# The odd slot of a cross-attention loop: the values' product moved ahead of the scores, its casts ahead of the odd tile's exponentials

## The chip, the cores and the metric

The kernel runs on one core of a Trainium2 chip. Five engines work side by side, each on its own queue of instructions in the order in which the program gives them: TensorE (PE in the profile, its weight loads PEld), VectorE (DVE), ScalarE (ACT), GpSimd (POOL) and SyncE (SP, which here only issues DMAs). An instruction that has to wait for another engine holds up everything behind it on its own queue. The metric is device microseconds of one execution.

## The reference

For each of 4 batches, 2048 rows of 512 numbers attend to a context of 77 rows with 16 heads of width 32; a mask drops context rows; the result is projected, added to the input and normalised.

```python
qs = (q @ wq)...; ks_ = (k @ wk)...; vs = (v @ wv)...        # k = v = context, heads of 32
scores = einsum('bhqd,bhkd->bhqk', qs, ks_) / sqrt(32)
scores = where(mask, -inf, scores)
attn = einsum('bhqk,bhkd->bhqd', softmax(scores), vs)
out = attn.reshape(...) @ wo + q
return (out - mean(out)) / sqrt(var(out) + 1e-5) * gamma + beta
```

Everything is float32.

## The kernel before

The 8192 rows are cut into 64 tiles of 128 rows; two tiles make a block (its number is n), and tile u = 2n is its even, u + 1 its odd tile. Products that need float32 accuracy are made of three float32r products: each operand is split into a high part (a cast on ScalarE) and a low part (the difference, on VectorE or GpSimd).

What happens to one tile, with the function and the engine:

- `q_visit` (L160, TensorE, 12 matmuls): one quarter of the queries of a group of four tiles; `q_evac` (L177, VectorE) copies it out. The rows come by `load_xT` (SP), are split by `cast_xT` (L149, ScalarE) and `split_xT` (L153, GpSimd).
- `scores` (L284, TensorE, 64 small matmuls): the 16 heads, in four PSUM banks j = 0 to 3 with four heads each. A head uses 32 rows and 64 columns of the array.
- `maxima` (L298, VectorE): mask and row maximum of one head, bank by bank (the list `HEADS` is ordered by j); writes the tile's buffer `pbuf`.
- `exps` (L312, ScalarE): the exponential of one head and its sum. `recip` (L323, VectorE): the reciprocals of the 16 sums. `normalise` (L328, GpSimd).
- `transp` (L352, VectorE) turns the tile within blocks of 32, `regroup` (L364, SP) moves a whole block with 12 DMAs into the tile `PT`.
- `av` (L382, TensorE, 32 matmuls on 96 rows and 32 columns of the array): the values' product of a block, in two banks `pa`. `av_hi` (L413, ScalarE, two casts) and `av_lo` (L417, VectorE, two differences) split it.
- `o_proj` (L446, TensorE, 12 matmuls): the projection of one tile; `residual` (L455), `moments` (L460, L465 on VectorE, L469 to L472 on GpSimd), `scale` (L478, ScalarE), `affine` (L482, L483, GpSimd), `store` (L486, SP).

The order of the work is written out by hand (the scheduler keeps it). A loop with `u = 0, 2, ..., 52` holds an even and an odd slot; tiles 54 to 63 follow a written list, `ORDER`, which the change doesn't touch. Stages are offset: while tile u is scored, block n - 2 goes through `av`, and tiles u - 6 and u - 5 through `o_proj`. So the order on TensorE is, for each pair: scores of u, `o_proj` of u - 6, a query visit; scores of u + 1, `av` of block n - 2, `o_proj` of u - 5, a query visit.

All PSUM tiles share eight banks. A bank is given out in the order in which banks came free in the program's text: a tile takes the bank whose last reader stands earliest, and TensorE waits for that reader. `AH`, `AL`, `PT` and the transposed tile `B` have two buffers each, `pbuf` has three.

The mask of the next batch is prepared in three pairs of the loop by `mask_bias` (L264, L265) and, one pair later, by `mask_nan` (L269 to L271), all on VectorE, at the end of the even slot.

Of the kernel before, what the change touches and what calls it, by code (L numbers as in the profile page):

```python
# [19 lines left out]
H = 16  # L20
# [47 lines left out]
def xattn_layernorm(  # L68
# [26 lines left out]
    def bank(name):  # L95
        return ps.tile([P, 512], F32, tag="mm", name=name)
# [37 lines left out]
    def keys_of(h):  # L134
        return slice(TAIL_K, NK2) if h % 2 == 0 else slice(0, NK)
# [6 lines left out]
    def load_xT(g, c):  # L142
        fx[g, c] = sb.tile([P, 2, GRP], F32, tag="xtf", name=f"xtf_{g}_{c}")
        nc.sync.dma_start(fx[g, c], xT[g, :, c : c + 2])
# [29 lines left out]
    def q_evac(g, m):  # L174
        pq = qp.pop((g, m))
        if g:
            nc.vector.tensor_copy(qd[g][:, m, :], pq)  # L177
        else:
            nc.vector.tensor_copy(qd[0][:, m : m + 2, BLK:], pq.rearrange("p (m r) -> p m r", m=2))
# [94 lines left out]
    def scores(t):  # L274
        qs = qd[t // 4]
        nmax[t] = sb.tile([P, H], F32, tag="nm", bufs=3, name=f"nm_{t}")
        sums[t] = sb.tile([P, H], F32, tag="sum", bufs=3, name=f"sum_{t}")
        sc = scs[t] = [bank(f"sc_{t}_{j}") for j in range(GH)]
        for g in range(NG):
            for half in range(0, P, P // 2):  # L280
                for j in range(GH):
                    q = slice(HD * j, HD * (j + 1))
                    r0 = (t % 4) * P + half
                    nc.tensor.matmul(  # L284
                        sc[j][half : half + P // 2, g * NK : (g + 1) * NK],
                        qs[q, g, r0 : r0 + P // 2],
                        kct[q, g, t // TPB, keys_of(j)],
                        start=True,
                        stop=True,
                    )  # L290

    def maxima(t, lo, hi):
        pb = pbuf[t % NPB]
        mb = bat[t // TPB][0]
        nm = nmax[t]
        for h in HEADS[lo:hi]:
            g, j = divmod(h, GH)
            nc.vector.tensor_tensor_reduce(  # L298
                pb[:, h // 2, (h % 2) * NK : (h % 2 + 1) * NK],
                scs[t][j][:, g * NK : (g + 1) * NK],  # L300
                mb[:, t % TPB, keys_of(h)],
                -1.0,
                3.0e38,
                ALU.add,
                ALU.min,
                accum_out=nm[:, h : h + 1],
            )

    def exps(t, lo, hi):
        pb = pbuf[t % NPB]  # L310
        for h in HEADS[lo:hi]:
            nc.scalar.activation(  # L312
                pb[:, h // 2, (h % 2) * NK : (h % 2 + 1) * NK],
                pb[:, h // 2, (h % 2) * NK : (h % 2 + 1) * NK],
                AF.Exp,
                bias=nmax[t][:, h : h + 1],
                scale=-1.0,
                accum_out=sums[t][:, h : h + 1],
            )

    def recip(t):
        ris[t] = sb.tile([P, H], F32, tag="ri", bufs=3, name=f"ri_{t}")
        nc.vector.reciprocal(ris[t], sums[t])  # L323
# [51 lines left out]
    def av(b):  # L375
        pt = pts[b].rearrange("p i a (q t r) -> p i a q t r", q=NP, t=2)
        for i in range(2):
            pas[b, i] = bank(f"pa_{b}_{i}")
        for g in range(NG):
            for j in range(GH):  # L380
                h = g * GH + j
                nc.tensor.matmul(  # L382
                    pas[b, g // 2][HD * j : HD * (j + 1), (g % 2) * BLK : (g % 2 + 1) * BLK],
                    vsb[:, 2 * b // TPB, HD * h : HD * (h + 1)],
                    pt[:NK2, :, h % 2, h // 2].rearrange("p i t r -> p t i r"),
                    start=True,
                    stop=True,
                )
# [16 lines left out]
    def at_part(b, k, i, by_tile):  # L405
        if by_tile:
            return at[b][k][:, :, i * P : (i + 1) * P], pas[b, i].rearrange("p (m r) -> p m r", m=NG)
        return at[b][k][:, 2 * i : 2 * i + 2], pas[b, i].rearrange("p (m r) -> p m r", m=2)

    def av_hi(b, i, by_tile=False):  # L410
        if b not in at:
            at[b] = [sb.tile([P, NG, BLK], F32R, tag=t, name=f"{t}_{b}") for t in ("AH", "AL")]
        nc.scalar.copy(*at_part(b, 0, i, by_tile))  # L413

    def av_lo(b, i, by_tile=False):
        hv, pv = at_part(b, 0, i, by_tile)
        nc.vector.tensor_tensor(at_part(b, 1, i, by_tile)[0], pv, hv.bitcast(F32), ALU.subtract)  # L417


    def load_x(t):  # L420
        if t < NT - 8:
            od[t] = sb.tile([P, D], F32, tag="o", bufs=8, name=f"o_{t}")
        elif t < NT - 4:
            if not ends:
                ends.append(sb.tile([P, NC_D, GRP], F32R, tag="xth", name="o_end").bitcast(F32))
            od[t] = ends[0][:, t % 4]
        else:
            if t % 2 == 0:
                ends.append(sb.tile([P, 2, GRP], F32, tag="xtf", name=f"o_end_{t}"))
            od[t] = ends[-1][:, t % 2]  # L430
        nc.sync.dma_start(od[t], x[t * P : (t + 1) * P, :])
# [148 lines left out]
    def pieces(u):  # L580
        return casts.get(u) or [((u + 8) // 4, u % 4)] * (u + 8 < 4 * NGRP)

    evac = [(0, 0)]
    for u in range(0, 2 * CUT, 2):
        n = u // 2
        m, k = divmod(u, TPB)

        for q in pieces(u + 2):
            if u >= 4:
                load_xT(*q)  # L590
        for t in (u - 4, u - 3):
            if t >= 0:
                load_x(t)
        scores(u)
        maxima(u, 0, H // 2)
        for q in evac:
            q_evac(*q)
        maxima(u, H // 2, H)
        for q in pieces(u):
            cast_xT(*q)  # L600
        exps(u, 0, 3 * H // 4)
        for v in list(vd):
            values_evac(v)
        for q in pieces(u):
            split_xT(*q)
        if u == 0:
            mask_bias(0, slice(1, TPB))
            split_wv()
        if u >= 6:
            o_proj(u - 6)  # L610
        for v in {2: (0,), 4: (2, 3)}.get(u, ()):
            values(v)
        for q in visits(u):
            q_visit(*q)
        if u >= 6:
            residual(u - 6)
            moments(u - 6)
        if u == 4:
            transp(2)
        if u:  # L620
            transp(u - 1)
            regroup(n - 1)
        if u >= 8:
            scale(u - 8)
            scale(u - 7)
        exps(u, 3 * H // 4, H)
        if u >= 8:
            affine(u - 8)
        for q in visits(u):
            q_evac(*q)  # L630
        if u == 0:
            load_wo()
            nc.gpsimd.memset(ident, 0.0)
            nc.gpsimd.affine_select(ident, ident, [[-1, P]], ALU.not_equal, 1.0, base=0, channel_multiplier=1)
        if u == 2:
            split_wo(0)
            split_wo(1)
        if k == TPB - 6 and m + 1 < NB:
            load_mask(m + 1)
        if k == TPB - 4 and m + 1 < NB:  # L640
            mask_bias(m + 1)
        if k == TPB - 2 and m + 1 < NB:
            mask_nan(m + 1)

        scores(u + 1)
        maxima(u + 1, 0, 3 * H // 4)
        recip(u)
        maxima(u + 1, 3 * H // 4, H)
        exps(u + 1, 0, H // 4)
        normalise(u)  # L650
        if u >= 8:
            affine(u - 7)
        for v in list(vd):
            values_evac(v)
        if u >= 4:
            av(n - 2)
            av_hi(n - 2, 0)
            av_hi(n - 2, 1)
        exps(u + 1, H // 4, H)
        if u >= 5:  # L660
            o_proj(u - 5)
        if u >= 4:
            av_lo(n - 2, 0)
        if u >= 5:
            residual(u - 5)
        if u >= 4:
            av_lo(n - 2, 1)
        if u != 2:
            transp(u)
        for v in {2: (1,)}.get(u, ()):  # L670
            values(v)
        evac = visits(u + 1)
        for q in evac:
            q_visit(*q)
        if u == 2:
            load_xT(*pieces(4)[0])
        if u >= 5:
            moments(u - 5)
        if u == 0:
            mask_nan(0)  # L680
        if u == 2:
            split_wo(2)
            split_wo(3)
        recip(u + 1)
        normalise(u + 1)
        if u >= 8:
            store(u - 8)
            store(u - 7)
# [87 lines left out]
```

## Time and profile before

| | us |
|---|---|
| median of 3 runs | 534.55 (533.18 to 534.91) |
| profiled execution, its time | 533.62 |
| profiled execution, its span | 531.8 |
| busy PE, DVE, ACT, POOL | 514.6, 485.3, 459.4, 401.1 |
| granted TensorE clock, mean | 0.996 |

A span runs from the first to the last instruction; the time has the launch around it. Instructions on one engine are pipelined, so one may start while the one before still shows as busy: for what a group costs in a full queue one takes the distance from its start to the start of the next group. "sc" is the tile of scores, "pq" queries, "po" projection, "pa" the values' product.

### The profile page before, as it was taken

The numbers are of one execution on the slowest core, as the hardware profiler recorded it, in microseconds if no ns is written. First come the engines' busy times: TensorE is split into PE (matmuls) and PEld (weight loads), VectorE is DVE, ScalarE is ACT, GpSimd is POOL, SyncE is SP. The second block draws the span as 40 slices with busy tenths as digits, with TensorE's granted clock in tenths as the row PEclk, the third lists the DMA queues.
The fourth block names the chain that finished last, engine by engine and source line by source line (L and its number), as shares of the span: only waits on it lengthen the run. The fifth ranks groups of instructions, "written<-read, shape, count | busy, mean of one in ns | idle before, by whom it ended". The sixth has DMA issues, their size and how long they took to land.

```text
span 531.8 us, 20432 instructions
## 1 busy us (share of the span) xinstructions
PE 514.6 (97%) x6858; PEld 393.0 (74%) x6858; DVE 485.3 (91%) x2592; ACT 459.4 (86%) x2215; POOL 401.1 (75%) x363
## 2 busy tenths in 40 slices
PE   8999999999999999999999999999999999998994
PEld 6977677777777777777777777777777777775672
DVE  5689889999999899889998998889999989999897
ACT  5687799998899999998899999998899999998500
POOL 0626537998799988887899888888799988665751
PEclk9999999999999999999999999999999999999998
DMA  8934757888778788887778788779777865859844
GB/s 303 403 119 110 216 148 183 234 210 221 212 185 219 216 226 211 217 208 206 200 201 226 206 222 220 190 188 254 188 201 215 229 187 160 220 141 272 230 135 158
DMA packets 58712, 110.24 MB, mean 207 GB/s; under 512 B 9392, under 2 KB 11056, under 8 KB 58608
## 3 DMA queue, kind: packets, MB, share of 16 engines
q1 hardware_dynamic: 55424, 102.64, 70.2%
q0 software_dynamic: 2304, 5.24, 3.5%
q10 hardware_dynamic: 880, 1.05, 0.8%
q8 instruction: 55, 0.90, 0.7%
q14 instruction: 49, 0.40, 0.2%
HBM read 41.79 MB, written 16.78 MB: 110 GB/s over the span
## 4 chain that ended last, share of the span: by engine, by line
PE 29%; ACT 28%; DVE 26%; DMA 9%; issue 3%; SPq 3%; POOL 1%; DVEq 0%; ACTq 0%
ACT pbuf L312 23%; PE po L446 10%; PE pq L160 9%; DVE pbuf L298 7%; DVE B L352 5%; DMA PT<-B 4%; PE pa L382 3%; PE sc L284 3%; DVE q L177 3%; DMA o<-x 3%; ACT AH L413 3%; SPq L364 2%; DVE st L460 2%; ACT o L478 2%; PE pk L186 1%
## 5 line engine op out<-in xcount | busy, mean ns | idle before, releaser
L312 ACT ACTIVATE pbuf<-pbuf,nm 128x77 f32<-128x77 f32 x1024 | 353.2, 356 | 30.0 <-DVE nm L298 24.8
L312 ACT ACTIVATION_READ_ACCUMULATOR pbuf<-pbuf,nm 128x1 f32 x1024 | 201.4, 197 | 0.0
L328 POOL TENSOR_TENSOR pbuf<-pbuf,ri 128x1232 f32<-128x1232 f32 x63 | 142.9, 2270 | 58.2 <-DVE ri L323 44.5
L298 DVE CUSTOM_DVE_ANT_0 pbuf<-sc,mb 128x77 f32<-128x77 f32 x1024 | 168.8, 230 | 3.1 <-PE sc L284 3.1
L446 PE MATMUL po<-woh,AH 128*128 128x512 f32 x256 | 108.6, 424 | 0.0
L446 PE MATMUL po<-wol,AH 128*128 128x512 f32 x256 | 100.2, 391 | 0.0
L446 PE MATMUL po<-woh,AL 128*128 128x512 f32 x256 | 100.1, 391 | 0.0
L160 PE MATMUL pq<-xth,wqh 128*128 128x512 f32 (+1 forms) x256 | 98.5, 385 | 0.1
L160 PE MATMUL pq<-xtl,wqh 128*128 128x512 f32 (+1 forms) x256 | 97.9, 382 | 0.0
L160 PE MATMUL pq<-xth,wql 128*128 128x512 f32 (+1 forms) x256 | 97.9, 382 | 0.0
L352 DVE STREAM_TRANSPOSE B<-pbuf 128x1280 f32<-128x1280 f32 x64 | 95.5, 1493 | 2.5 <-POOL pbuf L328 1.8
L298 DVE DVE_READ_ACCUMULATOR2_ANT nm<- 128x1 f32 x1024 | 84.3, 82 | 0.0
L284 PEld LDWEIGHTS sc<-kct,q 32*64 32x64 f32 x4096 | 51.9, 130 | 23.6 <-issue 16.5
L153 POOL TENSOR_TENSOR xtl<-xtf,xth 128x1024 fp32r<-128x1024 f32 x28 | 67.1, 2398 | 2.8 <-ACT xth L149 2.8
L382 PE MATMUL pa<-PT,vsb 96*32 96x256 f32 x992 | 60.2, 381 | 7.5 <-DMA o<-x 1.9
L483 POOL TENSOR_TENSOR o<-o,bet 128x512 f32<-128x512 f32 x48 | 63.2, 1316 | 3.8
L446 PEld LDWEIGHTS po<-woh,AH 128*128 128x128 f32 x256 | 48.0, 187 | 23.2 <-DVE nm L298 6.2
L284 PE MATMUL sc<-kct,q 32*64 32x77 f32 x4096 | 62.5, 238 | 0.4 <-DVE vsb L228 0.4
L482 POOL TENSOR_TENSOR o<-o,gam 128x512 f32<-128x512 f32 x48 | 61.8, 1287 | 0.6 <-ACT o L478 0.3
L446 PEld LDWEIGHTS po<-woh,AL 128*128 128x128 f32 x256 | 48.1, 188 | 10.9 <-DVE AL L417 0.3
L160 PEld LDWEIGHTS pq<-xth,wqh 128*128 128x128 f32 x256 | 48.1, 188 | 10.5 <-PE pq L160 0.5
L446 PEld LDWEIGHTS po<-wol,AH 128*128 128x128 f32 x256 | 48.2, 188 | 9.5 <-issue 1.4
(106 smaller groups left out, 670.9 us busy)
## 6 DMA issues: line engine op xcount, KB each, us to landing
PT<-B SPq DMA_DIRECT2D x346, 128.0 KB
xtf<-xT SPq DMA_DIRECT2D x28, 512.0 KB
o<-x SPq DMA_DIRECT2D x56, 256.0 KB
out<-o SPq DMA_DIRECT2D x56, 256.0 KB
PT<-B POOLq DMA_DIRECT2D x21, 128.0 KB, 5.1
o_end<-x SPq DMA_DIRECT2D x8, 256.0 KB
out<-o_end SPq DMA_DIRECT2D x8, 256.0 KB
xtf<-xT SPq DMA_DIRECT2D x4, 256.0 KB
```

Of the source, the lines that this page charges most:

```text
L153: nc.gpsimd.tensor_tensor(l, fx.pop((g, c)), h.bitcast(F32), ALU.subtract)
L160: nc.tensor.matmul(pq, w[:, c, m * P : (m + 1) * P], r[:, c, rs], start=(n == 0), stop=(n == 11))
L177: nc.vector.tensor_copy(qd[g][:, m, :], pq)
L284: nc.tensor.matmul(sc[j][half : half + P // 2, g * NK : (g + 1) * NK], qs[q, g, r0 : r0 + P // 2], kct[q, g, t // TPB, keys_of(j)], start= ...
L298: nc.vector.tensor_tensor_reduce(pb[:, h // 2, (h % 2) * NK : (h % 2 + 1) * NK], scs[t][j][:, g * NK : (g + 1) * NK], mb[:, t % TPB, keys_ ...
L312: nc.scalar.activation(pb[:, h // 2, (h % 2) * NK : (h % 2 + 1) * NK], pb[:, h // 2, (h % 2) * NK : (h % 2 + 1) * NK], AF.Exp, bias=nmax[t ...
L328: nc.gpsimd.tensor_tensor(pv, pv, rv.to_broadcast((P, NP, 2, NK)), ALU.mult)
L352: nc.vector.transpose(bt.rearrange("p c q r -> p q c r"), pbuf[t % NPB].rearrange("p q (c r) -> p q c r", c=5),)
L382: nc.tensor.matmul(pas[b, g // 2][HD * j : HD * (j + 1), (g % 2) * BLK : (g % 2 + 1) * BLK], vsb[:, 2 * b // TPB, HD * h : HD * (h + 1)], ...
L446: nc.tensor.matmul(pos[t], a[:, c, rs], w[:, c, :], start=(first and c == 0 and n == 0), stop=(c == NC_D - 1 and n == 2),)
L482: nc.gpsimd.tensor_tensor(o, o, gam, ALU.mult)
L483: nc.gpsimd.tensor_tensor(o, o, bet, ALU.add)
```

## The change

In the even slot the last four exponentials of tile u join the first twelve, ahead of the two `scale`s. In the odd slot `recip(u)` is the first thing on VectorE. On TensorE `av` goes ahead of the scores of tile u + 1 (it stood behind them), and `av_hi` on ScalarE stands ahead of all exponentials of tile u + 1 (four of them stood ahead of it). The two `av_lo` on VectorE stand behind the fourth and the eighth of the odd tile's maxima (they stood around `residual(u - 5)`). Nothing is added or removed, no DMA is moved, and the list for the last ten tiles is as it was.

```diff
         for q in pieces(u):
             cast_xT(*q)
-        exps(u, 0, 3 * H // 4)
+        exps(u, 0, H)
         for v in list(vd):
             values_evac(v)
...
             scale(u - 8)
             scale(u - 7)
-        exps(u, 3 * H // 4, H)
         if u >= 8:
             affine(u - 8)
...
+        recip(u)
+        if u >= 4:
+            av(n - 2)
+            av_hi(n - 2, 0)
+            av_hi(n - 2, 1)
         scores(u + 1)
-        maxima(u + 1, 0, 3 * H // 4)
-        recip(u)
-        maxima(u + 1, 3 * H // 4, H)
-        exps(u + 1, 0, H // 4)
+        maxima(u + 1, 0, H // 4)
+        if u >= 4:
+            av_lo(n - 2, 0)
+        maxima(u + 1, H // 4, H // 2)
+        if u >= 4:
+            av_lo(n - 2, 1)
+        maxima(u + 1, H // 2, H)
         normalise(u)
         if u >= 8:
             affine(u - 7)
         for v in list(vd):
             values_evac(v)
-        if u >= 4:
-            av(n - 2)
-            av_hi(n - 2, 0)
-            av_hi(n - 2, 1)
+        exps(u + 1, 0, H // 4)
         exps(u + 1, H // 4, H)
         if u >= 5:
             o_proj(u - 5)
-        if u >= 4:
-            av_lo(n - 2, 0)
         if u >= 5:
             residual(u - 5)
-        if u >= 4:
-            av_lo(n - 2, 1)
         if u != 2:
             transp(u)
```

## The prediction

> **What bounds the kernel now.** I read the page's busy line, then the busy times of the loop's settled part, then TensorE's instructions in order of time, and last the waits of that part.
>
> ```profile
> PE 514.6 (97%) x6858; PEld 393.0 (74%) x6858; DVE 485.3 (91%) x2592; ACT 459.4 (86%) x2215; POOL 401.1 (75%) x363
> ...
> 88.50:423.80 335.30, 330.76 (x4578) 254.68 (x4579) 312.74 (x1735) 318.20 (x1526) 293.36 (x244) 1.00 0.80 213
> ...
> 278.90 0.95 PE L284 MATMUL sc<-kct,q 32*64 32x77 f32 x64
> 279.78 0.51 PE L446 MATMUL po<-woh,AH 128*128 128x512 f32 x1
> ...
> 282.65 0.39 PE L160 MATMUL pq<-xth,wqh 128*128 128x512 f32 x1
> ...
> 285.14 0.39 PE L160 MATMUL pq<-xth,wql 128*128 128x512 f32 x1
> 285.46 0.95 PE L284 MATMUL sc<-kct,q 32*64 32x77 f32 x64
> 286.62 1.93 PE L382 MATMUL pa<-PT,vsb 96*32 96x256 f32 x32 [0.21 <-DMA o<-x]
> 288.49 0.50 PE L446 MATMUL po<-woh,AH 128*128 128x512 f32 x1
> ...
> 291.36 0.39 PE L160 MATMUL pq<-xth,wqh 128*128 128x512 f32 x1
> ...
> 294.17 0.95 PE L284 MATMUL sc<-kct,q 32*64 32x77 f32 x64
> ...
> L382 PE MATMUL pa<-PT,vsb 96*32 96x256 f32 x708 | 43.0, 381 | 4.7 <-DMA o<-x 1.9 <-DMA xtf<-xT 1.1 <-PE sc L284 0.9
> ```
>
> The second line (columns: window, length, busy PE, PEld, DVE, ACT, POOL, clock, DMA share, GB/s) begins at one `av` and ends at another, 22 pairs later: 335.3 / 22 = 15.24 us a pair. TensorE is busy for 330.76 of it, and the last row has all the rest: the only idle time of TensorE in 22 pairs is 4.7 us ahead of `av`, 0.2 each time, whatever landed meanwhile. ACT is busy 318.2 / 22 = 14.5 a pair, DVE 14.2, POOL 13.3, and the DMA engines 0.80 of the time. So TensorE sets the pace.
>
> **The steady pair.** From start to start the rows give: scores to projection 0.88, projection 2.87, query visit 2.81, scores to `av` 1.16, `av` 1.87, projection 2.87, query visit 2.81, together 15.27. `av` behind scores costs 0.28 more than a projection behind scores: the idle 0.21 and 0.07 of overlap. What it costs behind a query visit, and scores behind `av`, the list of the last tiles shows once:
>
> ```profile
> 438.62 0.39 PE L160 MATMUL pq<-xth,wql 128*128 128x512 f32 x1
> 438.93 1.93 PE L382 MATMUL pa<-PT,vsb 96*32 96x256 f32 x32
> 440.80 0.95 PE L284 MATMUL sc<-kct,q 32*64 32x77 f32 x64
> 441.68 0.50 PE L160 MATMUL pq<-xth,wqh 128*128 128x512 f32 x1
> ```
>
> From the last query matmul to `av` it is 0.31, where to scores it is 0.32 (285.14 to 285.46); `av` to scores takes 1.87, as `av` to projection does; no idle time is noted at either seam. The new pair is thus 0.88 + 2.87 + 2.81 + 1.87 + 0.88 + 2.87 + 2.81 = 14.99. Between both ends for the 0.28 (all of it gone; all of it moved to another seam) I take gone, by these rows. 23 `av` from 88.52 to 423.79 give 4.7 / 22 + 0.07 = 0.28 each: **-6.3 us**.
>
> A rule of the Trainium skill speaks against it: "TensorEngine Tiling (Array Packing)", section Tiling Modes, Key Properties, says that a change of tiling mode drains TensorE, and the new order has as many changes of mode (five a pair) as the old one. By that rule the sum would be 0 in place of -6.3; the rows at 438.93 and 440.80 show such changes with no idle time, so I keep it as a rival.
>
> **Do the other engines follow at 14.99?** I lay out a pair, with 0 at the start of the even scores; TensorE then starts `o_proj` at 0.9, the query visit at 3.7, `av` at 6.6, the odd scores at 8.4, `o_proj` at 9.3, the visit at 12.2. Prices:
>
> ```profile
> 428.72 0.69 DVE L455 TENSOR_TENSOR o<-po,o 128x512 f32<-128x512 f32 x1 [1.54 <-PE po L446]
> 429.33 0.68 DVE L417 TENSOR_TENSOR AL<-pa,AH 128x512 fp32r<-128x512 f32 x1
> 429.93 1.50 DVE L352 STREAM_TRANSPOSE B<-pbuf 128x1280 f32<-128x1280 f32 x1
> 431.35 0.65 DVE L460 BATCH_NORM_STATS2 st<-o 128x6 f32<-128x512 f32 x1
> 432.04 0.18 DVE L465 BATCH_NORM_AGGREGATE mv<-st 128x2 f32<-128x6 f32 x1
> 432.14 0.22 DVE L323 RECIPROCAL ri<-sum 128x16 f32<-128x16 f32 x1
> ...
> 432.61 0.36 ACT L312 ACTIVATE pbuf<-pbuf,nm 128x77 f32<-128x77 f32 x1 [0.61 <-DVE nm L298]
> ...
> L298 DVE CUSTOM_DVE_ANT_0 pbuf<-sc,mb 128x77 f32<-128x77 f32 x706 | 116.3, 230 | 0.0
> ...
> 407.54 1.41 ACT o L478 x2
> ...
> 411.69 0.95 ACT AH L413 x2
> 412.64 4.12 ACT pbuf L312 x24
> ...
> 420.78 2.40 POOL L153 TENSOR_TENSOR xtl<-xtf,xth 128x1024 fp32r<-128x1024 f32 x1
> 423.14 1.28 POOL L482 TENSOR_TENSOR o<-o,gam 128x512 f32<-128x512 f32 x1
> ...
> 428.20 1.29 POOL L482 TENSOR_TENSOR o<-o,gam 128x512 f32<-128x512 f32 x1
> ```
>
> A maximum is 116.3 / 706 = 0.16 (16 are 2.6), `residual`, `av_lo` or a query copy 0.6, `transp` 1.4, `moments` 0.8, `recip` 0.1; 16 exponentials are 4.12 x 16 / 12 = 5.5.
>
> VectorE, odd slot: maxima once the scores are through at 8.4 + 0.95 = 9.4; with the two `av_lo` 3.8, to 13.1; `residual` 13.7, `transp` 15.2, `moments` 16.0, `recip` 16.1, which is 1.1 in the next pair. Even slot: 2.6 + 0.6 + 0.6 + 0.8 + 1.4 + 0.6, so `recip(u)` comes up at 7.7. From there VectorE stands idle until 9.4, 1.7 us: the 1.54 that it waited for `residual` at 428.72, moved. `recip(u)`, now at the head, holds up the maxima behind it, but they wait for the scores anyhow.
>
> ScalarE: the first exponential comes 0.5 after `recip` (432.14 to 432.61), so `exps(u)` runs 1.4 to 6.9, so that `recip(u)` needn't wait; `scale` to 8.4, `av_hi` to 9.3 (its product was issued by 8.4), `exps(u + 1)` from 9.7 (the scores' 9.4 and one maximum) to 15.2, `cast_xT` 0.95 to 16.2 = 1.2. It fits, with 0.2 to spare.
>
> GpSimd: `affine(u - 8)` now waits for `scale` behind 16 exponentials instead of 12: 6.9 + 0.7 = 7.6, to 10.3 (2.65 by 423.14 and what follows it), `normalise(u)` to 12.5, ahead of `transp(u)` at 13.7. No queue but those of PE, ACT and DVE has its order changed.
>
> Banks: by the order in which banks come free, the scores of u + 2 take those of `scores(u + 1)` j = 0 and 1 and of the two `pa`; the last `av_lo` ends at about 12, need is at 15. `av` and the odd scores need `residual(u - 5)`, the last query copy and the maxima of u (done by 4.3). No wait. Three times in the loop `mask_bias` and, a pair later, `mask_nan` push VectorE back; these rows price them and the DMAs of `PT`:
>
> ```profile
> L265 DVE TENSOR_SCALAR mb<-m 128x304 bf16<-128x304 uint8 x3 | 4.2, 1394 | 0.0
> L264 DVE TENSOR_SCALAR mb<-m 128x1232 bf16<-128x1232 uint8 x3 | 3.8, 1255 | 0.0
> ...
> L269 DVE TENSOR_REDUCE nz<-m 128x16 f32<-128x1232 uint8 x3 | 4.2, 1415 | 0.0
> ...
> 272.49 7.86 SPq L364 DMA_DIRECT2D PT<-B  x12
> ...
> PT<-B POOLq DMA_DIRECT2D x21, 128.0 KB, 5.1
> ```
>
> `mask_bias` is 4.2 / 3 + 3.8 / 3 = 2.7; `mask_nan`, a reduction of 1.4 and two smaller instructions, I count at 2.7 too. Less the 1.7 that VectorE has idle, it falls back by 1.0 in the first pair and by 2.0 in the second, where the last `av_lo` ends at 14 instead of 12, inside the 15 by one microsecond. I take 0, and for the range 3 x 0.5, should these steps be a tenth too short. `PT`: SP issues its DMAs until 280.35, the `av` that reads it would start at 278.90 + 6.56 = 285.46. If the last one took as long as those on POOL's queue (5.1), it would land in that instant. I take 0 and give the range 1 us.
>
> **The first pairs.** At u = 4 `recip(4)`, now ahead of the maxima of tile 5, waits for late exponentials:
>
> ```profile
> 57.04 1.05 ACT L149 CAST xth<-xtf 128x1024 fp32r<-128x1024 f32 x1 [4.35 <-DMA xtf<-xT]
> ...
> 52.62 1.01 SPq L144 DMA_DIRECT2D xtf<-xT  x2
> ...
> 66.11 0.50 PE L446 MATMUL po<-woh,AH 128*128 128x512 f32 x1
> ...
> DVE B L352 <- POOL pbuf L328: 1.8, 1, 1.8
> ```
>
> They start at 58.0 and end at 63.5; the query visit behind the scores of 5 takes the bank that the first four maxima of 5 free, so it starts at 64.3, scores of 6 at 67.2, projection at 68.1 instead of 66.11; with the seam saved at the next `av` the loss is 1.7. Against it: `recip(0)` moves ahead of 12 maxima, so GpSimd's `normalise(0)`, for which VectorE waited 1.8, is through in time; `transp`, the DMAs behind it and the load at 52.62 come about 1.6 earlier, and the cast with them. I take 0; the range has -0.2 to +1.7.
>
> ```profile
> 431.33 0.95 PE L284 MATMUL sc<-kct,q 32*64 32x77 f32 x64
> ```
>
> **The end.** The list of the last ten tiles is as it was; TensorE, ScalarE and VectorE are all loaded there, so what counts is how late VectorE enters it. VectorE enters it at 1.1 after the scores of 54 started, where it did at 432.14 + 0.13 - 431.33 = 0.9: **+0.2**.
>
> Sum: -6.3 + 0 + 0 + 0.2 = -6.1. The profiled execution took 533.62 (span 531.8, 1.8 around it), so 527.5; the median of the runs is 0.93 above that execution, so **528.4**.
>
> **Rivals.** (a) The idle time only moves (to the seam between two narrow tilings, `av` to scores): 23 x 0.28 comes back, 534.55 + 0.2 = 534.8. For it: one row alone, 440.80, shows that seam without it. (b) Half of it: the first pairs cost 1.7, the mask pairs 1.5, `PT` 1: 528.4 + 1.7 to 4.2 = 530.1 to 532.6. (c) The other sign: VectorE becomes the bound. It is busy 14.2 a pair and has two waits at the head of its queue (`recip(u)` for ScalarE, the maxima for later scores). If its 1.7 idle at the odd scores comes on top of 14.2, a pair lasts 15.9, 0.66 more than now: +15, 550; it decides from 15.24 - 14.2 = 1.0 of idle that nothing makes up for, and midway it gives 540. Against it: that 14.2 counts overlaps and the mask, the steps above sum to 13.3, and the 1.54 wait at 428.72 goes in exchange.
>
> **How the numbers follow.** Forecast 0.60 (its own range 527.2 to 530), (b) 0.16, (a) 0.08, (c) 0.16. The lower end is all of the seams, the first pairs' 0.2 and the fastest run's 533.18: 533.18 - 6.5 = 526.7. Upward I go through (b) and (a) to 535.2, and leave out (c) and a little at the bottom. A difference under 0.3% (1.6 us) can't be told from none here: faster 0.76 (forecast and (b)), same 0.07, slower 0.17.
>
> **What would show it.** Right: no idle time noted ahead of `av` in the loop, pairs of 15.0 from scores to scores, VectorE's wait for `residual` gone and one ahead of the odd maxima in its place, released by TensorE's scores. Wrong: idle time at the scores behind `av` (a); waits of TensorE's scores on `av_lo` or maxima (b); pairs over 15.24 with VectorE or ScalarE without idle time (c).

## The result and the profile after

The changed kernel takes **530.75 us** (median of 4 runs, 530.03 to 531.31); the kernel before, run beside it, takes 534.36 (4 runs, 533.18 to 534.91). The ratio is 0.9935 (95% interval 0.9912 to 0.9957): 3.6 us faster, where 6.1 were forecast. It is faster, and by more than the 0.3% that can be told; the time lies inside the range of 526.7 to 535.2, and above the likeliest case's own 527.2 to 530.

The page after, its busy line and its granted clock in tenths:

```profile
PE 515.7 (97%) x6858; PEld 390.4 (74%) x6858; DVE 482.8 (91%) x2592; ACT 461.7 (87%) x2215; POOL 401.2 (76%) x363
...
PEclk9999999999999999999999999999999999997998
```

TensorE does the same work with 1.1 us more busy time, in a span that is 2.3 shorter. Where the 2.3 come from is seen when both executions are cut at the same points: the start of the scores of tiles 4, 8, 54 and 63. The columns of these windows are start and end, length, busy time of PE, PEld, DVE, ACT and POOL with their instructions, clock, DMA share and GB/s; first before, then after.

```profile
48.80:80.80 32.00, 31.33 (x417) 22.71 (x416) 28.70 (x167) 26.94 (x142) 15.40 (x7) 1.00 0.67 180
80.80:431.30 350.50, 345.80 (x4785) 266.21 (x4784) 326.18 (x1811) 333.40 (x1606) 305.11 (x254) 1.00 0.80 211
431.30:482.10 50.80, 50.56 (x826) 37.44 (x826) 50.49 (x321) 48.71 (x262) 36.92 (x39) 1.00 0.66 180
482.10:531.80 49.70, 39.61 (x345) 28.14 (x344) 43.27 (x118) 16.26 (x77) 24.98 (x42) 0.96 0.66 194
```

```profile
48.00:82.10 34.10, 31.56 (x417) 23.13 (x416) 28.09 (x158) 28.42 (x149) 13.77 (x6) 0.95 0.63 170
82.10:426.50 344.40, 344.40 (x4785) 262.28 (x4784) 322.32 (x1810) 332.23 (x1589) 304.13 (x253) 1.00 0.79 213
426.50:477.40 50.90, 50.47 (x828) 37.41 (x827) 50.57 (x321) 49.30 (x265) 37.48 (x40) 1.00 0.65 182
477.40:529.50 52.10, 42.47 (x345) 29.04 (x344) 43.57 (x119) 16.47 (x77) 24.99 (x42) 0.89 0.65 186
```

The 23 pairs of the loop are 6.1 us shorter (15.24 to 344.40 / 23 = 14.97 a pair), and TensorE has no idle time left in them: busy 344.40 of 344.40. The first pairs are 2.1 longer, at a clock of 0.95; the stretch behind the scores of 63 is 2.4 longer, at 0.89. Before, the clock is 1.00 in the first and 0.96 in the last of these (half clock in the last 3.8 us, where TensorE has nothing left). With 0.8 less ahead of the scores of 4 and 0.1 more in the list's first part that is the 2.3.

The seam itself, TensorE's instructions in order of time, in the pair that the prediction shows of before:

```profile
282.98 0.39 PE L160 MATMUL pq<-xth,wql 128*128 128x512 f32 x1
283.30 1.93 PE L382 MATMUL pa<-PT,vsb 96*32 96x256 f32 x32
285.16 0.95 PE L284 MATMUL sc<-kct,q 32*64 32x77 f32 x64
286.04 0.50 PE L446 MATMUL po<-woh,AH 128*128 128x512 f32 x1
```

From the last query matmul to `av` it is 0.32, from `av` to the scores 1.86, from them to the projection 0.88; no idle time is noted at any of them. And the waits of the settled part (88 to 424; us in all, times, longest):

```profile
DVE pbuf L298 <- PE sc L284: 18.5, 14, 1.5
...
POOL o L482 <- ACT o L478: 13.7, 23, 0.8
```

The same window of before had:

```profile
DVE o L455 <- PE po L446: 15.6, 12, 1.7
```

VectorE's wait for `residual` is gone, and one for the scores, about as long, stands ahead of the maxima. GpSimd's `affine` now waits for `scale`, as was laid out (13.7 us; before it was 0.3).

**The two losses.** Ahead of the query visit behind the scores of tile 5 TensorE now waits 2.54; before, none is noted there. The chain of waits around it:

```profile
50.65 4.39 DMA xtf<-xT
...
55.12 0.04 ACT xth L149
...
56.08 5.59 ACT pbuf L312 x32
...
61.69 0.04 DVE ri L323
...
61.86 0.19 DVE pbuf L298
...
62.67 3.55 PE pq L160 x10
```

The load lands, the cast follows, then 16 exponentials of tile 4, `recip(4)`, four maxima, and the bank is free. This is the chain that the prediction priced, and the load did come earlier, by 2.0 (50.65 for 52.62); 1.2 of that is against the scores of 4, which start 0.8 earlier themselves (48.00 for 48.81). What the prediction lacks is in TensorE's instructions behind the wait, there and ahead of `av(28)` in the list of the last tiles:

```profile
62.67 0.48 PE L160 MATMUL pq<-xth,wqh 128*128 128x512 f32 x1 [2.54 <-DVE nm L298]
...
63.68 0.41 PE L160 MATMUL pq<-xtl,wqh 128*128 128x512 f32 x1
63.91 0.60 PE L160 MATMUL pq<-xth,wql 128*128 128x512 f32 x1
64.31 0.63 PE L160 MATMUL pq<-xth,wqh 128*128 128x512 f32 x1
...
67.01 1.10 PE L284 MATMUL sc<-kct,q 32*64 32x77 f32 x64
...
480.14 3.49 PE L382 MATMUL pa<-PT,vsb 96*32 96x256 f32 x32 [1.83 <-DMA PT<-B]
483.56 2.08 PE L435 MATMUL po<-o,ident 128*128 128x512 f32 x2
...
487.39 0.39 PE L446 MATMUL po<-wol,AH 128*128 128x512 f32 x1
```

From 63.9 a matmul takes 0.40 to 0.43 from start to start where it took 0.23: the granted clock is 0.5 from 63.9 to 67.3, and again from 480.4 to 487.2. The visit takes 4.34 to the next scores, the `av` 3.42 to the next matmul instead of 1.86.

### The profile page after: what moved, and what is told of

Read it like the earlier page. It is cut to its first block, busy times and chain, and to the rows that moved or that the text cites. A ratio compares the mean times of both kernels' runs of the same rounds, so it can differ in the third digit from the quotient of the medians.

```text
span 529.5 us, 20454 instructions
## 1 busy us (share of the span) xinstructions
PE 515.7 (97%) x6858; PEld 390.4 (74%) x6858; DVE 482.8 (91%) x2592; ACT 461.7 (87%) x2215; POOL 401.2 (76%) x363
## 4 chain that ended last, share of the span: by engine, by line
PE 76%; DVE 8%; DMA 6%; SPq 4%; ACT 2%; issue 2%; POOL 1%; DVEq 0%; POOLq 0%; ACTq 0%
PE po L446 30%; PE pq L160 27%; PE pa L382 10%; PE sc L284 8%; DMA PT<-B 3%; SPq L364 3%; ACT pbuf L312 2%; DVE B L352 2%; DVE pbuf L298 2%; DMA stage_b<-wo 1%; DMA stage_a<-wk 1%; PE po L435 1%; DMA xtf<-xT 1%; DVE o_end L505 1%; DVE q L177 1%
## 5 line engine op out<-in xcount | busy, mean ns | idle before, releaser
L312 ACT ACTIVATION_READ_ACCUMULATOR pbuf<-pbuf,nm 128x1 f32 x1024 | 193.9, 189 | 0.0
L298 DVE CUSTOM_DVE_ANT_0 pbuf<-sc,mb 128x77 f32<-128x77 f32 x1024 | 170.7, 231 | 22.6 <-PE sc L284 22.6
L482 POOL TENSOR_TENSOR o<-o,gam 128x512 f32<-128x512 f32 x48 | 63.5, 1322 | 13.7 <-ACT o L478 13.7
L483 POOL TENSOR_TENSOR o<-o,bet 128x512 f32<-128x512 f32 x48 | 61.9, 1289 | 3.8
L382 PE MATMUL pa<-PT,vsb 96*32 96x256 f32 x992 | 61.5, 390 | 2.1 <-DMA PT<-B 2.1
L446 PEld LDWEIGHTS po<-woh,AH 128*128 128x128 f32 x256 | 48.2, 188 | 15.6 <-issue 2.1
```

What stands on the lines that cost most here:

```text
L298: nc.vector.tensor_tensor_reduce(pb[:, h // 2, (h % 2) * NK : (h % 2 + 1) * NK], scs[t][j][:, g * NK : (g + 1) * NK], mb[:, t % TPB, keys_ ...
L312: nc.scalar.activation(pb[:, h // 2, (h % 2) * NK : (h % 2 + 1) * NK], pb[:, h // 2, (h % 2) * NK : (h % 2 + 1) * NK], AF.Exp, bias=nmax[t ...
L382: nc.tensor.matmul(pas[b, g // 2][HD * j : HD * (j + 1), (g % 2) * BLK : (g % 2 + 1) * BLK], vsb[:, 2 * b // TPB, HD * h : HD * (h + 1)], ...
L446: nc.tensor.matmul(pos[t], a[:, c, rs], w[:, c, :], start=(first and c == 0 and n == 0), stop=(c == NC_D - 1 and n == 2),)
L482: nc.gpsimd.tensor_tensor(o, o, gam, ALU.mult)
L483: nc.gpsimd.tensor_tensor(o, o, bet, ALU.add)
```

## Experiments

All kernels were run beside the kernel before, on the same chip as it. A "stretch" below is cut at the same four starts of scores as above. The extra matmuls of e4, e6, e7, e9 and e10 are useless work into a bank that is overwritten, so the result stays the reference's.

**e1, `av` alone.** The kernel before with `av` ahead of the odd scores and nothing else.

```diff
+        if u >= 4:
+            av(n - 2)
         scores(u + 1)
...
         if u >= 4:
-            av(n - 2)
             av_hi(n - 2, 0)
```

> From the kernel before, only the values' product is moved ahead of the odd scores on TensorE; the orders of ScalarE and VectorE stay as they were before. Theory (the seam is the whole gain, and the new place of recip costs 2 us at u = 4): pairs of 14.97 as in the changed kernel, no wait of TensorE at u = 4, so about 2 us less than the changed kernel, 528.5. Rival (the casts and low parts have to be moved too, or VectorE or ScalarE falls behind by the 1.9 us that the odd scores come later): pairs of 15.1 or more, 531 or more.

**e2, all the rest.** The changed kernel with `av` and its casts behind the odd scores again.

```diff
         recip(u)
+        scores(u + 1)
         if u >= 4:
             av(n - 2)
             av_hi(n - 2, 0)
             av_hi(n - 2, 1)
-        scores(u + 1)
```

> The changed kernel, but the values' product stays behind the odd scores on TensorE, as before. Theory: pairs of 15.24 as before, the wait at u = 4 is there, 536. Rival (the gain comes from the orders of ScalarE and VectorE): pairs of 15.0 and 531.

Measured: `av` alone 528.72 us (528.21 to 529.17), ratio 0.9902 (0.9889 to 0.9915); the rest alone 535.19, ratio 1.0028 (1.0016 to 1.0041). The loop of the one and of the other, in the columns of above:

```profile
80.50:424.80 344.30, 343.93 (x4785) 262.08 (x4784) 326.87 (x1812) 331.79 (x1599) 303.76 (x253) 1.00 0.79 214
```

```profile
82.70:433.50 350.80, 346.19 (x4792) 266.57 (x4791) 326.73 (x1810) 334.01 (x1589) 304.98 (x253) 1.00 0.78 209
```

344.3 / 23 = 14.97 a pair, and 350.8 / 23 = 15.25. So the whole gain in the loop is the place of `av` on TensorE; the order of casts, low parts and exponentials gives nothing in the loop, and the loop didn't need it: with `av` alone the other engines kept up as well. In the second kernel the idle time still stands ahead of `av` behind scores, and is put down to something else each time:

```profile
288.65 1.93 PE L382 MATMUL pa<-PT,vsb 96*32 96x256 f32 x32 [0.18 <-DVE q L177]
```

The rest has a price in the first pairs: with it they take 34.19 (a wait of 2.14 at the query visit and 3.4 us of half clock), with `av` alone 31.73 (a wait of 0.86, where the expectation had none). And it has a worth outside the loop. From the scores of 54 to those of 63 it is 51.54 with `av` alone, against 50.83 in the changed kernel and 50.75 with the rest alone. VectorE's last `recip` of the loop, in the changed kernel and then with `av` alone:

```profile
427.48 0.22 DVE L323 RECIPROCAL ri<-sum 128x16 f32<-128x16 f32 x1
```

```profile
426.50 0.25 DVE L323 RECIPROCAL ri<-sum 128x16 f32<-128x16 f32 x1 [0.46 <-ACT pbuf L312]
```

That is 0.95 and 1.70 after the start of the scores of 54 (426.53 and 424.80): with `av` alone VectorE comes into the list 0.75 later, and the list's first part is 0.7 longer. Ahead of the loop the rest saves 0.3 more, between the scores of tiles 2 and 3 (9.30 for 9.62 before and 9.66 in e1). The end takes 51.05 with `av` alone and 49.20 with the rest alone, in one execution of each.

**e3, `recip(4)` back.** In the pair of tile 4 alone `recip` stands behind twelve maxima of tile 5, as before, and both `av_lo` behind all sixteen.

```diff
-        recip(u)
+        if u != 4:
+            recip(u)
...
+        if u == 4:
+            maxima(u + 1, 0, 3 * H // 4)
+            recip(u)
+            maxima(u + 1, 3 * H // 4, H)
             av_lo(n - 2, 0)
             av_lo(n - 2, 1)
+        else:
```

> The changed kernel, but in the one slot u = 4 recip stands behind 12 maxima of tile 5 again, the two low parts behind all 16. Theory (recip waits there for exponentials that a late load holds up, and TensorE waits 2.5 us behind it and then runs 3.4 us at half clock): scores of tile 8 start 3 us earlier against the start of scores of tile 4 than in the changed kernel, no clock of 0.5 near 64 us, 528.5. Rival (the wait at u = 4 is given back later by slack): 530.7 as the changed kernel.

Measured: 527.24 us (526.02 to 532.48), ratio 0.989 (0.9858 to 0.9922). The first pairs take 30.89 with a wait of 0.86 at the query visit: it is `recip(4)` at the head of VectorE's queue that carries the late load on to TensorE. The profiled execution is the slowest of its six. It has a wait of 2.66 ahead of the projection behind the scores of tile 9 (at 91.23), with half clock behind it, so that its loop takes 348.37, and an end of 52.18, with half clock too. What that projection waited for isn't shown: the profile names the maxima, but the bank that it takes was last read by `residual(2)`, through at 85.99. It isn't e3's edit alone either, for e12, whose loop is that of the changed kernel, has a wait of 1.02 at the same place (91.16).

**e5, the load earlier.** The load for which the cast of tile 4 waits is issued ahead of the regrouping of the block instead of behind it.

```diff
+            if u == 2:
+                load_xT(*pieces(4)[0])
             regroup(n - 1)
...
-        if u == 2:
-            load_xT(*pieces(4)[0])
```

> The changed kernel; the load of rows that cast_xT(4) reads is issued ahead of the 12 DMAs of regroup(0) on SyncE instead of behind them. Theory (at u = 4 the chain is late load, cast, exponentials, recip, maxima, bank, query visit): the cast of u = 4 starts about 5 us earlier, TensorE doesn't wait at u = 4, from scores of 4 to scores of 8 it is 30.5 to 31 instead of 34.1, 527.5. Rival (recip's place as such, not the load, makes the wait): 34 and 530.7.

Measured: 527.71 us (527.21 to 528.77), ratio 0.9872 (0.9849 to 0.9896). VectorE at the same place, in the changed kernel, then in this one, and TensorE in this one:

```profile
61.69 0.25 DVE L323 RECIPROCAL ri<-sum 128x16 f32<-128x16 f32 x1 [3.52 <-ACT pbuf L312]
```

```profile
58.56 0.23 DVE L323 RECIPROCAL ri<-sum 128x16 f32<-128x16 f32 x1
60.60 0.24 DVE L298 CUSTOM_DVE_ANT_0 pbuf<-sc,mb 128x77 f32<-128x77 f32 x1 [1.81 <-PE sc L284]
```

```profile
61.47 0.47 PE L160 MATMUL pq<-xth,wqh 128*128 128x512 f32 x1 [0.90 <-DVE nm L298]
...
64.40 0.95 PE L284 MATMUL sc<-kct,q 32*64 32x77 f32 x64
```

`recip(4)` no longer waits for the exponentials, VectorE waits for the scores instead, as in most pairs of the loop, and the first pairs take 30.94. The 0.90 that is left at the query visit was not expected. The visit stands right behind the scores there and takes the bank that the first four maxima of tile 5 free; e1, with `recip` in its old place, has 0.86 of it too.

**e4, the wait filled.** Eight useless matmuls go ahead of the real ones of `av(28)`, so that TensorE is busy where it waited for `PT`; the wait itself isn't shortened.

```diff
+        if b == 28:
+            for _ in range(8):
+                nc.tensor.matmul(pas[b, 0], woh[:, 0, :P], woh[:, 0, :], start=True, stop=True)
```

> The changed kernel with 8 matmuls of no use (1.8 us) ahead of the values' product of block 28, in the bank that it overwrites, where TensorE waited 1.83 us for the last DMAs of PT. Theory (that wait lets the clock fall to a half for 6.8 us, which costs some 2 us at the end): the clock stays at 1 there, 528.7. Rival (VectorE and the DMAs set the end, not TensorE's clock): 530.7, even where the clock stays up.

Measured: 529.51 us (527.34 to 530.95), ratio 0.9916 (0.9896 to 0.9936). TensorE around that `av`:

```profile
479.25 2.08 PE L381 MATMUL pa<-woh 128*128 128x512 f32 x8
481.26 1.93 PE L385 MATMUL pa<-PT,vsb 96*32 96x256 f32 x32
483.13 1.13 PE L438 MATMUL po<-o,ident 128*128 128x512 f32 x2
...
485.18 0.39 PE L449 MATMUL po<-wol,AH 128*128 128x512 f32 x1
```

The `av` has its 1.87 back, there is no half clock in the list, and from the scores of 63 to the end it is 49.34 instead of 52.17. In this execution the half clock stood at the first pairs (6.8 us of it, 35.64 in all). The median lies between the two answers of the expectation, and its interval overlaps that of the changed kernel: that the filled wait takes the half clock away is read from the profile, not from the time.

**e6 and e7, both, on the change and on `av` alone.** The early load and the filled wait, in the changed kernel and in that of e1.

> Both together, the early load and the 8 matmuls of no use ahead of the values' product of block 28. If the two losses are all that stood between the forecast and the time, they add: no clock of 0.5 before the last 10 us, loop as in the changed kernel, 525.0 to 526. If one eats the other: 527 or more.

> The kernel of e1 (only the values' product moved) with the same two additions. If the orders of ScalarE and VectorE are worth nothing, the same time as e6, 525 to 526; if moving the casts and low parts gives something at the end of the loop, 0.5 to 1 us more than e6.

Measured: 526.68 us (526.29 to 527.31), ratio 0.9852 (0.9829 to 0.9874), and 528.4 (526.60 to 530.79), ratio 0.9882 (0.9857 to 0.9907). No half clock in either profile ahead of the last microseconds. e6 lies between its two answers: its end is still 50.79, 1.0 above before, so half clock isn't all of the loss there. Against e6, e7 is 1.7 slower, though its end is shorter (49.85). That is the second answer: with the early load the orders of ScalarE and VectorE are worth something. In the profiles 0.7 of it stands in the list's first part (51.51 for 50.83), where e1 lost it too. The intervals of the two ratios overlap, so the 1.7 is a likely figure and not a sharp one.

**e8, the changed kernel once more.**

> The changed kernel once more, for its spread: if the clock falls to a half in some executions and not in others, the times spread over 2 us or more and go with the mean clock; before spread over 2.3 us in 14 runs with clocks of 0.995 to 0.997 in all but one.

Measured: 530.31 us (528.41 to 531.49, 6 runs), ratio 0.9919 (0.9894 to 0.9943). The times spread over 3.1 us. This profiled execution has the waits without half clock behind them: 1.96 at the first query visit, and the first pairs take 32.09, as before (32.02). Yet the end takes 51.56, 1.8 more than before. TensorE's waits there, and a piece of the chain:

```profile
478.24 1.93 PE L382 MATMUL pa<-PT,vsb 96*32 96x256 f32 x32 [1.38 <-DMA o_end<-x]
486.45 1.93 PE L382 MATMUL pa<-PT,vsb 96*32 96x256 f32 x32 [1.43 <-DMA o_end<-x]
496.23 1.93 PE L382 MATMUL pa<-PT,vsb 96*32 96x256 f32 x32 [1.26 <-DMA PT<-B]
```

```profile
474.25 6.44 DMA PT<-B
480.76 5.38 DMA o_end<-x
486.15 0.59 ACTq L364
```

The chain goes through the loads of `x` for the last tiles (`o_end`), which the list issues between the regrouping DMAs that `av` waits for. The `x` of tiles 58 to 63 is first used behind the regrouping of block 30, which these loads stand ahead of.

**e9 to e12, those loads later.** The loads of `x` for tiles 58 to 63 (1.5 MB) are issued behind the regrouping DMAs of block 30 (all but one, on GpSimd's queue) and ahead of those of block 31, which is the last: in the kernel with the early load and the filled wait, which was run again beside it, and then in the kernel before and in the changed kernel with nothing else.

```diff
-... P29.3s x58 x59 T62.2 ... V28 e62.3 P29.4g x60 x61 z50 ... b28.1 x62 x63 P30.8g ... P30.11g P30.1s e62.1
+... P29.3s T62.2 ... V28 e62.3 P29.4g z50 ... b28.1 P30.8g ... P30.11g P30.1s x58 x59 x60 x61 x62 x63 e62.1
```

> The changed kernel with the early load and the useless matmuls ahead of av(28) (as e6), and in the list of the last tiles the loads of x for tiles 58 to 63 (6 x 256 KB = 1.5 MB) are issued behind the regrouping DMAs of the last block instead of between them. Theory A (in the last 50 us the av of blocks 29 and 30 wait for the DMAs of PT because the DMA engines are full): 1.5 MB at 215 to 238 GB/s are some 6.5 us of the DMA engines' time taken out from ahead of PT, so av 30 starts 1 to 3 us earlier than e6's 70.5 us after the scores of tile 54, the waits ahead of av(29) and av(30) are gone, and the stretch from the scores of 63 to the end falls from e6's 50.79 to 49.3 - 50.0; median 525.2 to 526.2. Theory B (av 29 and 30 wait for the engines that make PT's source, and the full DMA engines only go along with it): av 30 stays at 70 to 71 and the stretch at 50.5 to 51.2; median 526.4 to 527.

> The same kernel as e6, for the spread of one kernel's end between executions and to stand beside e9 on the same chip: 526.3 to 527.3, the stretch from the scores of 63 to the end 50.5 to 51.2, no half clock before the end. If a spell of half clock shows, or the stretch is under 50, then e6's 50.79 was one of several ends that this kernel has.

> The kernel before, with nothing but the loads of x for tiles 58 to 63 issued behind the regrouping DMAs of the last block. If the full DMA engines cost the kernel before as much as the changed one, its stretch from the scores of 63 to the end falls from 49.78 by 1.2 to 2 like that of e6 to e9 (to 47.8 - 48.6) and the median to 532.5 - 533. If the changed kernel alone pays there (it comes to the end with later or slower DMAs), the stretch falls by under 0.7 (its waits there were 0.98, 0.94 and 0.38, and are gone) and the median stays within 533.3 - 534.3.

> The changed kernel with nothing but these six loads issued later. The waits ahead of av(29) and av(30) go as in e9; the one ahead of av(28) has four of the six loads still behind it, and stays at 1.3 to 1.9 us, with the half clock behind it or without it: from the scores of 63 to the end 50.0 to 50.6 without (51.6 to 52.2 with it) in place of 51.6 to 52.2; the first tiles as in the changed kernel (34.1, or 32.1 without half clock). Median 528.7 to 529.5.

| kernel | median us (runs) | ratio (interval) | 4 to 8 | end |
|---|---|---|---|---|
| e9, loads later | 525.19 (524.76 to 525.26) | 0.9831 (0.9813 to 0.9848) | 30.93 | 49.17 |
| e10, without that | 526.57 (525.88 to 527.41) | 0.9859 (0.9838 to 0.9879) | 30.97 | 51.21 |
| e11, before with loads later | 532.59 (531.79 to 534.25) | 0.9969 (0.9951 to 0.9986) | 31.80 | 48.68 |
| e12, changed with loads later | 527.55 (526.25 to 528.99) | 0.9877 (0.9854 to 0.9899) | 32.25 | 48.79 |

Eight microseconds from just after the scores of 63 on, in the columns of above; in turn of before, of the changed kernel run again, and of e12:

```profile
483.30:491.30 8.00, 6.74 (x48) 3.98 (x48) 7.30 (x29) 6.09 (x34) 4.02 (x6) 1.00 1.06 264
```

```profile
476.90:484.90 8.00, 6.66 (x48) 3.97 (x48) 6.98 (x30) 5.62 (x31) 3.93 (x5) 1.00 1.06 251
```

```profile
478.00:486.00 8.00, 6.99 (x56) 4.17 (x60) 7.24 (x29) 6.34 (x34) 3.96 (x6) 1.00 0.62 146
```

With the loads where they were, the DMA engines are full (share 1.06) in both; without them they are not (0.62), the waits ahead of `av(29)` and `av(30)` are gone, and both kernels come to the end alike: 48.68 and 48.79. The wait ahead of `av(28)` stays in both (1.14 and 1.31). So the end's loss comes from these loads. SyncE's queue around the last regrouping DMAs of block 29, in the changed kernel run again and then in e12:

```profile
476.80 1.55 SPq L431 DMA_DIRECT2D o_end<-x  x2
479.70 0.59 SPq L364 DMA_DIRECT2D PT<-B  x1
```

```profile
475.00 3.49 SPq L364 DMA_DIRECT2D PT<-B  x5
```

The loads act in two ways. They stand ahead of the last of these DMAs, so that SyncE is through with them 4.5 us after the scores of 63 started instead of 1.7. And the DMAs behind them take longer: the six of block 30 on GpSimd's queue, issued at about the same time (from 9.4 and from 9.2 us after the scores of 63), land in 6.4 to 7.9 us with the loads ahead and in 3.2 to 5.6 without. In the kernel before these take 5.1 to 7.1, and 3.2 to 5.6 with the loads later. How much of `av(29)`'s wait belongs to either isn't separated.

The kernel before paid for it too (1.1 us), the changed one more (2.8 against its second execution). e9 came out as its theory A had it (49.17 and 525.19, each just under its range), e10 as e6 did. The expectation for e11 had 1.2 to 2 for one answer and under 0.7 for the other; 1.1 lies between, nearer the first: both pay, and not the same. That for e12 was too high, 50.0 to 50.6 and 528.7 us or more. Why the changed kernel pays more isn't settled. Full engines moved 251 GB/s in it and 264 before, but e4, with the same fast loop, lost nothing (49.34).

With these loads later in both kernels the change is worth 532.59 - 527.55 = 5.0 us on one chip, of the 6.1 that were forecast. In the two profiles the loop gives 5.9 (351.08 and 345.19, the wait of 1.02 at tile 9 included) and the first pairs take back 0.5.

The kernel e9 beats both: 8.6 us under the kernel before on the same chip, and by the ratios 1% (some 5 us) under the changed one. What the eight useless matmuls are worth in it wasn't run by itself.

## Why the prediction was right, and where it was off

- **The steady pair, -6.3 us.** Right: 14.99 forecast, 14.97 measured, -6.1 over the 23 pairs. The step that chose between "gone" and "moved" by a single row (440.80) held in every pair, and e1 and e2 tie it to the place of `av` alone. Rival (a) falls with it. (By its own 0.28 for each of 23 `av` the term would be 6.4; nothing hangs on the 0.1.) The rule of the Trainium skill named there ("TensorEngine Tiling (Array Packing)", section Tiling Modes, Key Properties: a change of mode drains TensorE) gives no idle time in these traces at the seams from query visit to `av` and from `av` to scores, with as many changes of mode as before; the trace decides. Start to start, a change to or from the full array does show: 0.32 from the last query matmul to `av` as to scores, and 0.34 for the first matmul of a projection behind scores (286.04 to 286.38), where it is 0.23 between like matmuls. That stands in both kernels equally often. Whether it is the drain, and what the 0.2 behind the scores was, these runs don't show.
- **The other engines.** Right: no pair got longer, VectorE's idle time moved to the odd maxima as laid out (18.5 us for 15.6), and rival (c) found nothing to feed on: TensorE is never idle in the loop of either profile of the changed kernel. e1 shows more than was asked: the casts' new places weren't needed for it.
- **Mask pairs and `PT`, 0 each.** Right: no idle time of TensorE in the loop.
- **The first pairs, 0, range -0.2 to +1.7.** The chain was right step by step (late load, `recip(4)`, maxima, bank), and so was what set it off, the load 2.0 earlier where 1.6 was said (1.2 against the scores of 4). The sum was right when only the waits count: +0.1 in the changed kernel's second execution, +0.2 in e12, both against 32.02. It was off by 2.1 in the first, 0.4 past the range's end. A longer wait (2.54 for 1.96) is 0.6 of that; the larger part is one that the step has nothing for, what a wait does to the clock behind it: 4.34 for a query visit that takes 2.93 in e5 (61.47 to the scores at 64.40), +1.4.
- **The end, +0.2.** This is the step that failed: "what counts is how late VectorE enters it". It holds up to the scores of 63: `recip(53)` starts 0.95 after the scores of 54 for 0.81 before, and that part is 0.1 longer (50.83 for 50.73); with `av` alone VectorE enters 0.75 later and the part is 0.7 longer. Behind the scores of 63 it measured +2.4, and +1.8 without half clock. The step looked at three loaded engines and left the fourth resource out, the DMA engines, which are all but full from 5 us ahead of the scores of 63 (share 1.01 before, 0.98 after). With the loads out of the way the step is right: 48.79 against 48.68, +0.1. And as at the first pairs, a wait of 1.83 had half clock behind it: `av(28)` to the first low matmul of the projection behind it takes 480.14 to 487.39 after, and 481.26 to 485.18 in e4, 3.3 us more; the waits that then fall away give part of it back.
- **The sum.** -6.1 forecast, -3.6 by the medians. Of the 2.5 that are missing the loads at the end are the larger part (1.8 - 0.2 = 1.6, by one profile). The half clock, which one profiled execution of the changed kernel has and the other has not, is a candidate for the rest, and not a shown one. Of the six runs of e8 the two with a mean clock of 0.995 and 0.996 took 528.41 and 529.12 and the four with 0.992 to 0.994 took 530.10 to 531.49; but of the first four runs one with 0.997 took 531.16. That the time lies in the forecast's range is owed to the range's upper part, which was drawn for other losses. Rival (b) gave 530.1 to 532.6 and so the right time. Of its three terms the mask pairs and `PT` in the loop cost nothing, and the first pairs cost 2.1 in one execution and 0.1 in the other; the end isn't among them. The time doesn't confirm it.

## What to carry to other kernels

An idle seam of 0.28 us that is noted in every pair, whatever landed meanwhile, goes by the order on its own engine: move that one group alone before rearranging its neighbours. Here the neighbours gave nothing in the loop; they gave 0.7 us behind it and 0.3 ahead of it, and in the first pairs they cost 0.4 to 2.4 until the late load was moved. Before a faster loop is added up, look at the stretch behind it for what is full there, DMA engines included, and move out of it what nobody waits for yet. Price a new wait of TensorE with the clock behind it: a wait of about 2 us can cost 1.4 to 3.3 us more.

## What the runs showed of the hardware

**Half clock behind a short wait.** Ahead of the last microseconds the granted clock was 0.5 for 3.4 or for 6.8 us, and only at single waits of TensorE: in the profiles of before, the changed kernel and these experiments at waits of 1.83 (6.8 us), 1.86, 2.14, 2.54 and 2.66 (3.4 each) and 2.83 (6.8). No wait up to 1.54 had it, and neither did 1.96 (e8) and 2.18 (e12): between them it isn't the length of the wait alone. The Trainium skill ("TensorE: Matmul & The Clock Gate", Part 1) has a window of some 3.4 us that runs free of the kernel and sets the clock, and the spells agree with one or two of them; its rule there speaks of idle gaps of over some 3.4 us, where in these traces waits of 1.83 and more were enough; the traces decide.

**Full DMA engines at different rates.** At a share of 1.06 the same stretch of the list moved 264 GB/s before, 251 and 245 in the two executions of the changed kernel, and 275 in e4 (8.0 us from 479.5), with the same loads in it. In the four executions with the wait ahead of `av(28)` filled and the loads in their old place the end falls as the rate rises: 51.21 at 243 (e10), 50.79 at 252 (e6), 49.85 at 267 (e7), 49.34 at 275 (e4). What makes the difference is open.
